# A two-block image kernel with a selective scan: one odd multiply in 16 on VectorE, a later read-out, earlier projection inputs

## The chip, the cores and the metric

The kernel runs on one core of a Trainium2 chip. The metric is the device time of one execution in microseconds; a time is the median of several executions. The engines are TensorE (PE, and PEld for its weight loads), VectorE (DVE), ScalarE (ACT), GpSimd (POOL) and SyncE (SP), which here issues every DMA. Each works through its own instructions in the order of the program, and they meet at semaphores.

## The reference, cut to what matters

Sixteen images of 64 x 64 positions and 96 channels go through two residual blocks, each behind a group norm. The first block resamples, squares and projects. The second one is a selective scan over the 4096 positions, in four directions, of 192 channels with 16 states each:

```python
def step(h, inps):
    dt, ut, bt, ct = inps
    h = jnp.exp(dt[..., None] * As[None]) * h + (dt * ut)[..., None] * bt[:, :, None, :]
    y = jnp.einsum('bkdn,bkn->bkd', h, ct)
    return (h, y)
...
x_dbl = jnp.einsum('bkdl,kcd->bkcl', xs, x_proj_weight)
dts, Bs, Cs = jnp.split(x_dbl, [R, R + N], axis=2)
dts = jnp.einsum('bkrl,kdr->bkdl', dts, dt_projs_weight)
As = -jnp.exp(A_logs).reshape(K, d, N)
ys = selective_scan(xs, dts, As, Bs, Cs, Ds.reshape(K, d), dt_projs_bias)
```

`dt` passes through a softplus first. The whole is in fp32.

## The kernel before, in words

**Three generators around one loop.** `front` (L240) is all that stands ahead of an image's scan: block one, group norms, the depthwise convolution, and the stores of the scan's inputs xs to DRAM. `finish` (L510) is what follows it: norm, gate, output projection. Both are Python generators; each `yield` ends a slice of work. `front(0)` runs by itself before the scan and `finish(15)` after it; all others are woven into the scan loop of another image, slice by slice.

**The scan.** `scan` (L606) goes through 128 steps: 16 images of 8 steps, a step being one pair of directions (forward or backward) and one quarter (T = 1024) of the positions. A step has 6 blocks of 4 pairs, so 24 pairs n; 3072 in all. A pair has two groups, e = 1 (odd) and e = 0 (even), each of 32 channels x 4 states on the 128 partitions. For each pair the loop (from L833 on) issues:

- `recur(n, 1)`: VectorE scans the odd group, reading the decay `da` from PSUM and the drive `b` from SBUF, and writes h over `b` (L740 forward, L742 backward).
- `keep(n, 1)`: ScalarE copies the last column of h for the next quarter (L748; not in the last quarter of a direction).
- `decay(n + 1, 1)`: ScalarE makes the next odd decay in PSUM (L725; two buffers of 128 x 1024 in PSUM, one of each parity).
- `read_out(n - 1)`: TensorE adds both groups of the pair before into y, 16 matmuls (L764), and with the first pair of a block of a backward step also what the forward step left (y0, L757).
- slot 0; then POOL multiplies the odd h by ct in place (L877), and `drive(n + 2)`: POOL multiplies dtu by bt for both groups of the pair after next (L731), into one of three buffers `b`.
- `recur(n, 0)`: VectorE scans the even group, h into PSUM over `da`; slot 1; VectorE multiplies it by ct from PSUM into `b` (L887); `keep(n, 0)`, `decay(n + 1, 0)`, slot 2.

When a block of 4 pairs is over, `store` (L769) copies y out by ScalarE and issues its store.

**The slots.** In each of the three slots of a pair the `Background` class takes at most one slice of two generators: the projection of the next step, and `front` of the next image or, when that is done, `finish` of the last one. Rates are set by SLICES, PSLICES and the number of positions (L72 to L75): the projection goes on by about one slice for each slot, so its 58 slices fill about pairs 0 to 19 of a step. Nothing but program order decides: an instruction of a slice that waits holds up all that its engine has behind it.

**The projection.** `project` (L622) makes the step sizes of the next step in two halves of TB = 512 columns. It loads three tiles u (L634, three buffers), waits three slots, multiplies them into pp (PE, L640), one slot later copies that to pr (ACT, L643), and then goes through three chains, in the order v = 0, 2, 1: s by a matmul (L650), softplus in ScalarE and VectorE (L658 to L669), dtu = s x u[v] (DVE, L672), a copy to delta (ACT, L674), and the stores of dtu and delta to DRAM (L676, L677). `fetch` (L679) loads these again, spread over the partitions, in two buffers each, a block ahead of their use; `fetch_bc` loads bt and ct.

**Other places the change touches.** In `front`, the resampled image s returns from DRAM in two tiles, of 44 and 20 columns, that have SBUF pools of their own (b18 and b12), by six loads (L415), before the loop whose matmuls (L433) use it. In the loop, y0 is fetched (L867, L702; one buffer) in the second pair of a block for the first pair of the next.

Of the kernel before, what the change touches and what calls it, by code (L numbers as in the profile page):

```python
# [45 lines left out]
F32 = mybir.dt.float32  # L46
# [25 lines left out]
SLICES = 540  # L72
WAIT = -1
# [5 lines left out]
def tile_two_blocks(  # L79
# [103 lines left out]
    b12 = ctx.enter_context(tc.tile_pool(name="b12", bufs=1))  # L183
# [56 lines left out]
    def front(mi):  # L240
# [72 lines left out]
        for p0 in range(0, UPS, PP):  # L313
# [94 lines left out]
        JS = 44  # L408
        s = [
            b18.tile([UPS, JS, C], F32, name="s0", tag="b18"), b12.tile([UPS, HW - JS, C], F32, name="s1", tag="b12")  # L410
        ]
        for _ in range(2):
            yield
        for i, n, first in [(0, JS // 4, k * JS // 4) for k in range(4)] + [(1, 10, 0), (1, 10, 10)]:
            nc.sync.dma_start(out=s[i][:, first:first + n, :], in_=s_d[:, JS * i + first:JS * i + first + n, :])  # L415
            yield
# [4 lines left out]
        for j0 in range(0, HW + 8, 8):  # L421
            if done is not None:
                nc.scalar.activation(
                    x1v[:, :, j0 - 8:j0], done.rearrange("c w h -> c h w"), AF.Identity, bias=shift
                )
            if j0 < HW:
                done = bank([C, 8, HW], "e_ps")
                nc.tensor.matmul(
                    done.rearrange("c w h -> c h w"), lhsT=lin, rhs=x1v[:, :, j0:j0 + 8], start=True, stop=False,
                    skip_group_check=True,  # L430
                )
                for j in range(8):
                    nc.tensor.matmul(  # L433
                        done[:, j, :], lhsT=s[(j0 + j) // JS][:, (j0 + j) % JS, :], rhs=down_s, start=False, stop=True,
                        skip_group_check=True,
                    )
            yield
# [168 lines left out]
    def scan():  # L606


        with ExitStack() as es:
# [3 lines left out]
            p3 = es.enter_context(tc.tile_pool(name="sc_3", bufs=3))  # L613
# [8 lines left out]
            def project(mi, pair, lc, out):  # L622
# [6 lines left out]
                xs_d = image[mi]["xs"]  # L629
                for t in range(0, T, TB):  # L630
                    u = []
                    for v in range(3):
                        uv = up_.tile([128, TB], F32, name="u")
                        nc.sync.dma_start(out=uv, in_=xs_d[v, :, lc * T + t:lc * T + t + TB])  # L634
                        u.append(uv)
                    for _ in range(3):
                        yield
# [3 lines left out]
                    yield  # L641
# [4 lines left out]
                    for i, v in enumerate((0, 2, 1)):  # L646
# [30 lines left out]
                        nc.sync.dma_start(out=out["delta"][v][:, t:t + TB], in_=delta)  # L677

            def fetch(what, ctx, bi):  # L679

                v, s0, r = blocks[bi]
                t = p2.tile([128, 2, T], F32, name=what)
                for e in (1, 0):
                    nc.sync.dma_start(
                        out=t[:, e, :],
                        in_=ctx[what][v][32 * (s0 + e):32 * (s0 + e) + 32, :].unsqueeze(1).to_broadcast([32, NQ, T]),
                    )
                return t
# [39 lines left out]
            def drive(n):  # L728
                b = p3.tile([128, 2, T], F32, name="b")
                bt = bc[0, blocks[units[n][1]][2], units[n][2]]  # L730
                nc.gpsimd.tensor_mul(b, ops["dtu", n // NQ], bt.unsqueeze(1).to_broadcast([128, 2, T]))  # L731
                bs[n] = b
# [11 lines left out]
            def keep(n, e, h):  # L744
                st, bi, j = units[n]
                if st % NT < NT - 1:
                    end = h[:, T - 1:T] if steps[st][1] == 0 else h[:, 0:1]
                    nc.scalar.copy(states[bi][1][:, e, j:j + 1], end)  # L748
# [84 lines left out]
            for n, (st, bi, j) in enumerate(units):  # L833
# [19 lines left out]
                if j == 0:  # L853
                    ahead = None
                    if bi + 1 < len(blocks):
                        ahead = ctxs[st], bi + 1
                    elif n + NQ <= last:
                        step_gen.drain()
                        ahead = ctxs[st + 1], 0
                    if ahead:  # L860
                        ops["dtu", m + 1] = fetch("dtu", *ahead)
                elif j == 1:
                    if ahead:
                        ops["delta", m + 1] = fetch("delta", *ahead)
                    if n + NQ <= last and steps[units[n + NQ - 1][0]][1] == 1:
                        st2, bi2, _ = units[n + NQ - 1]
                        y0s[steps[st2][2], bi2] = fetch_y0(steps[st2][2], bi2)  # L867

                h = bs[n][:, 1, :]
                recur(n, 1, h)  # L870
                keep(n, 1, h)
                if n < last:
                    decay(n + 1, 1)
                if n:
                    read_out(n - 1)
                slot(0)
                nc.gpsimd.tensor_mul(h, h, bc[1, r, j])  # L877
# [9 lines left out]
                nc.vector.tensor_mul(bs[n][:, 0, :], h, bc[1, r, j])  # L887
                keep(n, 0, h)
# [16 lines left out]
            read_out(last)  # L905
# [112 lines left out]
```

## Time and profile before

| | |
|---|---|
| median of 3 runs | 21,913.98 us (21,904.93 to 21,924.91) |
| profiled execution | 21,910.69 us |
| its span, first to last instruction | 21,908.9 us |
| POOL, DVE, PE, ACT busy | 95%, 91%, 70%, 60% |
| first and last start of L731 on POOL | 513.3 us and 21,735.6 us |
| DMA traffic | 4276.30 MB, mean 195 GB/s |
| mean granted TensorE clock | 0.766 |

A line of the groups reads: source line, engine, operation, what it writes and from what, shapes and count; then the busy time in us, the mean duration of one in ns, the idle time of the engine just before these instructions, and what ended most of it. A line of the waits reads: who waited, for whom, us in total, how often, and the longest. A line of the timeline reads: start in us, duration, engine, line, instruction, count, and in brackets the idle time before it with its releaser. SPq is the queue of SyncE, where a DMA is issued.

### The profile page before, as it was taken

Reading aid. Unit: us, or ns where it says so; the run is one execution under the profiler, and the core shown is the slowest. Engines: PE = TensorE matmul, PEld = TensorE weight load, DVE = VectorE, ACT = ScalarE, POOL = GpSimd, SP = SyncE. Lnnn points to the kernel's source line nnn. Section 1 sums busy time; section 2 is a strip of 40 time slices with the busy share of each in tenths; the row PEclk is TensorE's granted clock in tenths of the full one; section 3 lists DMA queues with packets and bytes.
Section 4 is the critical chain, followed back from the end, with each engine's and each line's share of the span. In section 5 each row is a group of like instructions: output and inputs, shape, how many; then the busy total and the mean of one; then the engine's idle time right before and its main releaser. Section 6 shows DMA issues by size and latency. Waiting matters only on the chain.

```text
span 21908.9 us, 260666 instructions
## 1 busy us (share of the span) xinstructions
PE 15342.2 (70%) x92844; PEld 6324.7 (29%) x92844; DVE 19849.9 (91%) x12829; ACT 13130.2 (60%) x20854; POOL 20900.4 (95%) x6152
## 2 busy tenths in 40 slices
PE   6766767766777677777767677767777677677745
PEld 4322323232232322324233232322323223242211
DVE  0999999999999999999999999999999999999996
ACT  4665656666565665656656566665656656566543
POOL 0999999999999999999999999999999999999997
PEclk7776777877778777777877778777787877778856
DMA  2555565656656566565655656556565655656654
GB/s 80 190 191 188 193 214 194 209 195 200 205 191 215 189 206 201 192 215 192 207 198 194 214 192 209 196 201 206 193 211 189 210 199 198 206 195 208 210 177 134
DMA packets 1851895, 4276.30 MB, mean 195 GB/s; under 512 B 449118, under 2 KB 548350, under 8 KB 1848542
## 3 DMA queue, kind: packets, MB, share of 16 engines
q1 hardware_dynamic: 1850590, 4259.62, 58.1%
q8 instruction: 731, 11.98, 0.2%
q14 instruction: 574, 4.70, 0.1%
HBM read 3380.58 MB, written 878.18 MB: 194 GB/s over the span
## 4 chain that ended last, share of the span: by engine, by line
DVE 36%; POOL 19%; issue 18%; PE 9%; ACT 9%; DMA 7%; SPq 1%; POOLq 0%; DVEq 0%; ACTq 0%
POOL b L731 10%; POOL b L877 10%; DVE da L742 7%; DVE da L740 7%; DVE b L740 6%; DVE b L742 6%; DVE b L887 4%; ACT da L725 4%; DMA u<-xs_d 2%; DVE s L669 2%; DVE dtu L672 2%; DVE s L668 2%; PE y L764 1%; DMA ct<-rows 1%; PE pp L640 1%
## 5 line engine op out<-in xcount | busy, mean ns | idle before, releaser
L731 POOL TENSOR_TENSOR b<-dtu,bt 128x2048 f32<-128x2048 f32 x3072 | 13984.9, 4552 | 584.6 <-DMA dtu<-dtu_d 522.9
L725 ACT ACTIVATE da<-delta,a_s 128x1024 f32<-128x1024 f32 x6144 | 6853.5, 1116 | 2826.6 <-DVE b L887 1185.9
L877 POOL TENSOR_TENSOR b<-b,ct 128x1024 f32<-128x1024 f32 x3072 | 7309.1, 2379 | 259.8 <-ACT new L748 249.5
L764 PE MATMUL y<-b,fold_s 128*32 128x256 f32 x49152 | 4638.9, 492 | 4107.3 <-DVE b L887 3102.6
L887 DVE TENSOR_TENSOR b<-da,ct 128x1024 f32<-128x1024 f32 x3072 | 3752.6, 1222 | 84.5
L764 PEld LDWEIGHTS y<-b,fold_s 128*32 128x32 f32 x49152 | 1353.3, 126 | 7627.7 <-DVE b L887 4083.3
L740 DVE TENSOR_TENSOR_SCAN da<-da,new,b 128x1024 f32<-128x1024 f32 x1152 | 2694.3, 2339 | 252.3 <-ACT da L725 252.3
L740 DVE TENSOR_TENSOR_SCAN b<-da,new,b 128x1024 f32<-128x1024 f32 x1152 | 2698.0, 2342 | 174.1 <-POOL b L731 166.9
L742 DVE TENSOR_TENSOR_SCAN da<-da,new,b 128x1024 f32<-128x1024 f32 x1152 | 2693.8, 2338 | 172.9 <-ACT da L725 172.7
L742 DVE TENSOR_TENSOR_SCAN b<-da,new,b 128x1024 f32<-128x1024 f32 x1152 | 2697.1, 2341 | 151.6 <-POOL b L731 109.5
L748 ACT COPY new<-da 128x1 f32<-128x1 f32 x2304 | 362.3, 157 | 3028.5 <-DVE b L887 3023.2
L473 PE MATMUL c_ps<-xgp,wtap_s 96*128 96x512 f32 (+1 forms) x4608 | 1817.8, 675 | 168.9 <-ACT row L491 164.1
L650 PE MATMUL s<-pr,dtw_s 128*128 128x512 f32 x1536 | 1120.4, 819 | 557.8 <-ACT delta L674 516.7
L377 PE MATMUL o_ps<-w2c_s,hsq 128*100 128x96 f32 x9600 | 1205.3, 293 | 191.9 <-ACT hsq L348 180.1
L365 PE MATMUL h_ps<-xu,w1t_s 96*128 96x500 f32 x1920 | 1147.6, 700 | 244.2 <-ACT hsq L348 108.6
L748 ACT COPY new<-b 128x1 f32<-128x1 f32 x2304 | 432.6, 188 | 1445.7 <-DVE b L742 740.4
L377 PEld LDWEIGHTS o_ps<-w2c_s,hsq 128*100 128x100 f32 x9600 | 1119.5, 203 | 407.4 <-ACT hsq L348 227.7
L640 PE MATMUL pp<-u,xpt_s 128*128 128x512 f32 x1536 | 903.7, 734 | 224.2 <-DMA u<-xs_d 216.0
L742 DVE TENSOR_TENSOR_SCAN b<-da,b 128x1024 f32<-128x1024 f32 x384 | 876.7, 2283 | 133.2 <-ACT da L725 74.8
L473 PEld LDWEIGHTS c_ps<-xgp,wtap_s 96*128 96x128 f32 (+1 forms) x4608 | 631.9, 182 | 1193.3 <-issue 938.6
L740 DVE TENSOR_TENSOR_SCAN da<-da,b 128x1024 f32<-128x1024 f32 x384 | 875.8, 2281 | 106.9 <-ACT da L725 106.9
L742 DVE TENSOR_TENSOR_SCAN da<-da,b 128x1024 f32<-128x1024 f32 x384 | 876.0, 2281 | 105.0 <-ACT da L725 105.0
(120 smaller groups left out, 18077.1 us busy)
## 6 DMA issues: line engine op xcount, KB each, us to landing
dtu<-dtu_d SPq DMA_DIRECT2D x1536, 512.0 KB
delta<-delta_d SPq DMA_DIRECT2D x1536, 512.0 KB
bt<-rows SPq DMA_DIRECT2D x1024, 512.0 KB
ct<-rows SPq DMA_DIRECT2D x1024, 512.0 KB
u<-xs_d SPq DMA_DIRECT2D x896, 256.0 KB
dtu_d<-dtu SPq DMA_DIRECT2D x768, 256.0 KB
delta_d<-delta SPq DMA_DIRECT2D x768, 256.0 KB
xr<-in_x SPq DMA_DIRECT2D x768, 128.0 KB
```

Source lines behind the costliest of these rows:

```text
L365: nc.tensor.matmul(h_ps[j], lhsT=w1t_s[:, 128 * j:128 * (j + 1)], rhs=xu.rearrange("c p q -> c (p q)"), start=True, stop=True,)
L377: nc.tensor.matmul(o_ps[:, p, :], lhsT=hsq[j][:, UPS * p:UPS * (p + 1)], rhs=w2c_s[:, j, :], start=(j == 0), stop=(j == HB - 1),)
L473: nc.tensor.matmul(c_ps[p:p + n], lhsT=wtap_s[:, tap, 128 * i:128 * i + n], rhs=xgp[:, h0:h0 + 8, dx:dx + HW], start=(tap == 0), stop=(tap ...
L640: nc.tensor.matmul(pp, lhsT=xpt_s[:, pair, v, :], rhs=u[v], start=(v == 0), stop=(v == 2))
L650: nc.tensor.matmul(s, lhsT=dtw_s[:, pair, v, :], rhs=pr, start=True, stop=True)
L725: nc.scalar.activation(da, ops["delta", n // NQ][:, e, :], AF.Exp, scale=a_s[:, k, g, units[n][2]:units[n][2] + 1])
L731: nc.gpsimd.tensor_mul(b, ops["dtu", n // NQ], bt.unsqueeze(1).to_broadcast([128, 2, T]))
L740: nc.vector.tensor_tensor_scan(out, da, b, before, ALU.mult, ALU.add)
L742: nc.vector.tensor_tensor_scan(out[:, ::-1], da[:, ::-1], b[:, ::-1], before, ALU.mult, ALU.add)
L764: nc.tensor.matmul(y[32 * q:32 * q + 32, e, :], lhsT=fold_s, rhs=b[:, e, QT * q:QT * q + QT], start=(pair == 0 and j == 0 and e == 0), sto ...
L877: nc.gpsimd.tensor_mul(h, h, bc[1, r, j])
L887: nc.vector.tensor_mul(bs[n][:, 0, :], h, bc[1, r, j])
```

## The change

In every sixteenth pair (n mod 16 = 15) the odd scan writes h into PSUM, as the even one does, and VectorE multiplies it by ct from there; POOL does it in the other 15. `read_out` and `store` come a pair later (n - 2), with four buffers `b` in place of three. In `project`, the loads of u for the first half are issued at the start, four slots ahead of pp; for the second half each tile is loaded at the end of the chain that used its buffer, and pp follows directly after the last of these; pr comes two slots after pp. The y0 fetch moves to the last pair of the block before. In `front` s comes as 40 and then 24 columns through one buffer, which frees the pool b12. `fetch` issues its two DMAs through a new helper, `spread`; its two buffers were there before. `keep` takes the copying function as an argument, always ScalarE's.

```diff
+SHARE = 16
...
-    b12 = ctx.enter_context(tc.tile_pool(name="b12", bufs=1))
...
+        def fetch_s(first, n):
+            t = b18.tile([UPS, n, C], F32, name="s", tag="b18")
+            for k in range(0, n, 8):
+                nc.sync.dma_start(out=t[:, k:k + 8, :], in_=s_d[:, first + k:first + k + 8, :])
+                yield t, first
+
+        JS = 40
         for _ in range(2):
             yield
-        for i, n, first in [(0, JS // 4, k * JS // 4) for k in range(4)] + [(1, 10, 0), (1, 10, 10)]:
-            nc.sync.dma_start(out=s[i][:, first:first + n, :], in_=s_d[:, JS * i + first:JS * i + first + n, :])
+        for s, s_first in fetch_s(0, JS):
             yield
...
+            if j0 == JS:
+                for s, s_first in fetch_s(JS, HW - JS):
+                    yield
+                for _ in range(2):
+                    yield
...
-            p3 = es.enter_context(tc.tile_pool(name="sc_3", bufs=3))
+            p4 = es.enter_context(tc.tile_pool(name="sc_4", bufs=4))
...
+                order = (0, 2, 1)
+
+                def fetch_u(v, t):
+                    uv = up_.tile([128, TB], F32, name="u")
+                    nc.sync.dma_start(out=uv, in_=xs_d[v, :, lc * T + t:lc * T + t + TB])
+                    return uv
+
+                ahead_u = [fetch_u(v, 0) for v in order]
+                for _ in range(4):
+                    yield
                 for t in range(0, T, TB):
-                    u = []
-                    for v in range(3):
-                        uv = up_.tile([128, TB], F32, name="u")
-                        nc.sync.dma_start(out=uv, in_=xs_d[v, :, lc * T + t:lc * T + t + TB])
-                        u.append(uv)
-                    for _ in range(3):
-                        yield
+                    u, ahead_u = dict(zip(order, ahead_u)), []
                     pp = gps.tile([128, TB], F32, name="pp", tag="g")
                     for v in range(3):
                         nc.tensor.matmul(pp, lhsT=xpt_s[:, pair, v, :], rhs=u[v], start=(v == 0), stop=(v == 2))
-                    yield
+                    for _ in range(2):
+                        yield
                     pr = pj.tile([128, TB], F32, name="pr")
...
                         nc.sync.dma_start(out=out["delta"][v][:, t:t + TB], in_=delta)
+                        if t + TB < T:
+                            ahead_u.append(fetch_u(v, t + TB))
...
-                    if n + NQ <= last and steps[units[n + NQ - 1][0]][1] == 1:
-                        st2, bi2, _ = units[n + NQ - 1]
-                        y0s[steps[st2][2], bi2] = fetch_y0(steps[st2][2], bi2)
-
-                h = bs[n][:, 1, :]
+
+                odd_here = n % SHARE == SHARE - 1
+                h = das[n, 1] if odd_here else bs[n][:, 1, :]
                 recur(n, 1, h)
-                keep(n, 1, h)
+                if odd_here:
+                    nc.vector.tensor_mul(bs[n][:, 1, :], h, bc[1, r, j])
+                keep(n, 1, h, nc.scalar.copy)
                 if n < last:
                     decay(n + 1, 1)
-                if n:
-                    read_out(n - 1)
+                if n >= 2:
+                    read_out(n - 2)
                 slot(0)
-                nc.gpsimd.tensor_mul(h, h, bc[1, r, j])
+                if not odd_here:
+                    nc.gpsimd.tensor_mul(h, h, bc[1, r, j])
                 if n + 2 <= last:
                     drive(n + 2)

                 h = das[n, 0]
                 recur(n, 0, h)
-                if n and units[n - 1][2] == NQ - 1:
-                    storing = store(n - 1)
+                if n >= 2 and units[n - 2][2] == NQ - 1:
+                    storing = store(n - 2)
                     next(storing)
...
+                if j == NQ - 1 and n < last and steps[units[n + 1][0]][1] == 1:
+                    st2, bi2, _ = units[n + 1]
+                    y0s[steps[st2][2], bi2] = fetch_y0(steps[st2][2], bi2)
```

More of the change, by code (lines that the diff above doesn't have):

```diff
@@ L405, in front @@
         stow(sd, UPS - 2 * PG)
[L408 to L411, printed above, removed]
+        def fetch_s(first, n):
[4 more added lines that the diff above has]
+        JS = 40
         for _ in range(2):
             yield
-        for i, n, first in [(0, JS // 4, k * JS // 4) for k in range(4)] + [(1, 10, 0), (1, 10, 10)]:
-            nc.sync.dma_start(out=s[i][:, first:first + n, :], in_=s_d[:, JS * i + first:JS * i + first + n, :])
+        for s, s_first in fetch_s(0, JS):
             yield
@@ L433, in front @@
                     nc.tensor.matmul(
-                        done[:, j, :], lhsT=s[(j0 + j) // JS][:, (j0 + j) % JS, :], rhs=down_s, start=False, stop=True,
+                        done[:, j, :], lhsT=s[:, j0 + j - s_first, :], rhs=down_s, start=False, stop=True,
                         skip_group_check=True,
@@ L640, in project @@
                         nc.tensor.matmul(pp, lhsT=xpt_s[:, pair, v, :], rhs=u[v], start=(v == 0), stop=(v == 2))
-                    yield
+                    for _ in range(2):
+                        yield
                     pr = pj.tile([128, TB], F32, name="pr")
                     nc.scalar.activation(pr, pp, AF.Identity, bias=bumps_s)
-                    for i, v in enumerate((0, 2, 1)):
+                    for i, v in enumerate(order):
                         if i == 0:
@@ L677, in project, with spread @@
                         nc.sync.dma_start(out=out["delta"][v][:, t:t + TB], in_=delta)
+                        if t + TB < T:
+                            ahead_u.append(fetch_u(v, t + TB))
+            def spread(out, what, ctx, bi, e):
+                v, s0, r = blocks[bi]
+                nc.sync.dma_start(
+                    out=out,
+                    in_=ctx[what][v][32 * (s0 + e):32 * (s0 + e) + 32, :].unsqueeze(1).to_broadcast([32, NQ, T]),
+                )
             def fetch(what, ctx, bi):
-                v, s0, r = blocks[bi]
                 t = p2.tile([128, 2, T], F32, name=what)
                 for e in (1, 0):
[L684 to L687, printed above, removed]
+                    spread(t[:, e, :], what, ctx, bi, e)
                 return t
@@ L728, in drive @@
             def drive(n):
-                b = p3.tile([128, 2, T], F32, name="b")
+                b = p4.tile([128, 2, T], F32, name="b")
                 bt = bc[0, blocks[units[n][1]][2], units[n][2]]
@@ L742, in recur, with keep @@
                     nc.vector.tensor_tensor_scan(out[:, ::-1], da[:, ::-1], b[:, ::-1], before, ALU.mult, ALU.add)
-            def keep(n, e, h):
+            def keep(n, e, h, copy):
                 st, bi, j = units[n]
@@ L747, in keep @@
                     end = h[:, T - 1:T] if steps[st][1] == 0 else h[:, 0:1]
-                    nc.scalar.copy(states[bi][1][:, e, j:j + 1], end)
+                    copy(states[bi][1][:, e, j:j + 1], end)
             def read_out(n):
@@ L887, in scan @@
                 nc.vector.tensor_mul(bs[n][:, 0, :], h, bc[1, r, j])
-                keep(n, 0, h)
+                keep(n, 0, h, nc.scalar.copy)
                 if n < last:
@@ L904, in scan @@
                         bc[what, 0, ahead_j] = fetch_bc(ctxs[st + 1], 0, ahead_j, what)
-            read_out(last)
+            for n in (last - 1, last):
+                read_out(n)
             for _ in store(last):
```

## The prediction

> **What bounds the kernel now.** I read the busy table first, then the costliest groups, then the waits by engine, then the timeline of one projection.
>
> ```profile
> PE 15342.2 (70%) x92844; PEld 6324.7 (29%) x92844; DVE 19849.9 (91%) x12829; ACT 13130.2 (60%) x20854; POOL 20900.4 (95%) x6152
> ...
> L731 POOL TENSOR_TENSOR b<-dtu,bt 128x2048 f32<-128x2048 f32 x3072 | 13984.9, 4552 | 584.6 <-DMA dtu<-dtu_d 522.9
> ...
> L877 POOL TENSOR_TENSOR b<-b,ct 128x1024 f32<-128x1024 f32 x3072 | 7309.1, 2379 | 259.8 <-ACT new L748 249.5
> ...
> L887 DVE TENSOR_TENSOR b<-da,ct 128x1024 f32<-128x1024 f32 x3072 | 3752.6, 1222 | 84.5
> ```
>
> GpSimd (POOL) is 95% busy, VectorE (DVE) 91%. In the timeline POOL's starts follow each other by 4.49 us after a drive (L731) and 2.31 us after a multiply (L877): 6.80 us for a pair, 163.2 us for the 24 pairs of a step. The scan runs from POOL's first drive at 513.3 us to its last multiply at 21,745.4 us: 21,232 us, or 165.9 us for each of 128 steps. POOL's waits after its start (the page's 844 us less the 512.3 us before the first drive) are some 320 us, 2.5 a step. So POOL sets the pace, but VectorE is only a little behind, as its waits tell:
>
> ```profile
> DVE da L740 <- ACT da L725: 359.2, 285, 5.9
> ...
> DVE da L742 <- ACT da L725: 277.6, 267, 2.4
> ...
> DVE b L740 <- POOL b L731: 216.8, 270, 1.1
> DVE b L742 <- POOL b L731: 166.5, 198, 1.1
> DVE b L742 <- ACT da L725: 114.8, 90, 1.5
> ```
>
> Only 216.8 + 166.5 = 383 us (3.0 a step) of VectorE's idle time is a wait for POOL. ScalarE (ACT) is waited for longest: with the projection's own small waits some 920 us inside the scan (7.2 a step). Laid out by place in the step, the waits for POOL stand in pairs 0 to 3, where no projection runs; in pairs 4 to 20 VectorE trails by 1 to 4 us. POOL's 249.5 us for L748 are also ACT's lateness: the end states of those scans were copied 3.7 us late at the median, where 0.2 us is usual.
>
> The next fence, of one step, shows how an ACT wait arises:
>
> ```profile
> 5052.51 0.59 ACT L674 COPY delta<-s 128x512 f32<-128x512 f32 x1 [0.93 <-DVE dtu L672]
> ...
> 5053.51 2.77 SPq L634 DMA_DIRECT2D u<-xs_d  x3
> ...
> 5064.26 4.90 PE L640 MATMUL pp<-u,xpt_s 128*128 128x512 f32 x6 [5.98 <-DMA u<-xs_d]
> ...
> 5069.19 0.69 ACT L643 ACTIVATE pr<-pp,bumps_s 128x512 f32<-128x512 f32 x1 [4.01 <-PE pp L640]
> ...
> 5074.27 2.36 DVE L740 TENSOR_TENSOR_SCAN da<-da,new,b 128x1024 f32<-128x1024 f32 x1 [3.52 <-ACT da L725]
> ```
>
> The three u tiles were issued behind the delta store and landed about 10.7 us after the first issue. TensorE (PE) stood at pp, pr (ACT) stood 4.01 us, and the even group's scan lost 3.52 us. Over all 768 loads u lands 6.7 us after its issue at the median (5.1 to 9.0 for the middle 80%); the DMA share in this stretch is 0.95.
>
> [...]
>
> **The change, part by part.**
>
> 1. *Odd multiply, 192 of 3072 pairs.* POOL loses 192 x 2.31 = 443 us (3.5 a step). VectorE gains 192 x 1.222 = 235 us (1.8 a step). The multiply runs before the even scan, so that scan and all of VectorE's queue stand 1.22 us later, and at that place POOL gets 2.31 + 1.22 = 3.5 us closer to VectorE. The PSUM buffer is held 1.22 us longer; its next decay (1.12 us) still has 2.34 + 1.22 us before it is needed: nothing. Were VectorE to take over as the bound at once, with ACT's waits unchanged, the most that is left is 383 - 235 = 148 us. Part of the 383 will stay, since in pairs 20 to 3 VectorE (5.9 us a pair of its own) outruns POOL's 6.8: 8 x 0.9 = 7.2 us to catch up, of which the lag now takes about 3 and, with POOL 3.5 us closer, up to 4.5. I keep 1.0 us a step, 128 us (bounds 0 and 190). Gain: 20 us (148 down to -42).
>
> 2. *Read-out two pairs back, four buffers.* PE no longer stops at read_out for L887 (3102.6 us of idle PE) and L877 (989.8). PE has room, so this counts only where ACT then waits for PE and VectorE for ACT. For every ACT-caused wait of VectorE I looked 7 us back for a wait of ACT on PE: 198 us stand behind pr, 80 behind the projection's s, 103 behind the other background matmuls; 509 us have no such wait, ACT is simply full, and stay. Of the 80 + 103 = 183 I take 155 (bounds 60 and 300, the latter with pr). The drive still needs the buffer whose read-out stands in the same pair of the program, so POOL does not get further ahead.
>
> 3. *u a chain ahead.* For the first half of a step four slots instead of three, and pr two slots after pp: its wait goes. That wait (118 of the 198 us) stands in pair 2, where VectorE otherwise waits for POOL: nothing. For the second half only two of the three tiles come early. The third chain's load stands behind the last delta store, with pp directly after it: no slot between where there were three, and pr two slots on instead of four. Relative to the end of pair 10's odd scan the delta copy moves from -5.2 us (pair 9) to about +1.9 (it is then queued behind a decay), the issue is at +2.3, the landing at +2.3 + 6.5 = 8.8, and the remaining four pp matmuls (4.90/6 = 0.82 us each after a wait, 0.59 otherwise) end at 11 to 12. Pr's place comes at +7.0, as now. So ACT stands 4 to 5 us where the mean is now 0.8. In the steps of now where pr stood 3.5 to 3.9 us the next even scan lost 3.0 to 3.5; over all steps it loses 1.15 there. Cost: 2.1 us a step, 270 us (bounds 40, if the load lands in some 4 us, and 450, if the read-out queued behind pp holds drives too).
>
> 4. *Step sizes.* They were in two buffers before (bufs=2); the new helper issues the same two DMAs: nothing, up or down.
>
> 5. *y0 fetch at the pair before its use.* SP waited 128.7 us for its buffer and no longer will; SP runs ahead. Nothing (bounds -20 and +20).
>
> 6. *The s image in 40 + 24 columns of one buffer.* Fifteen of 16 times beside the scan. Before the scan once: a second load with nothing beside it, about 6 us (first load: issued at 259.0, used at 263.5, with 15.4 us of waits). SP's queue stands behind it, two pairs at most. Four slots more for an image, of some 520 in 540: fits.
>
> Sum against the profiled execution's 21,910.7 us (span 21,908.9 and 1.8 around it): -20 - 155 + 270 + 6 = +101, so 22,012 us. The median of the runs shown is 21,914.0, 3 us above the profiled one, less than I can tell.
>
> **Rivals.**
>
> - *Faster.* The third load lands under cover and the freed PE gives most of its waits back: -148 + 64 (half a step's residue) - 250 + 60 + 6 = -268, so 21,643 us. One mechanism decides: whether u of the last chain lands within 4.5 us of its issue; then pr is in time. For it: two thirds of the competing u loads are gone by then. Against it: landings of 6.7 us and a DMA share of 0.95.
> - *Even.* Stall of 1.5 us a step (190) and all 183 back: -20 - 183 + 190 + 6 = -7: 21,904 us.
> - *Much slower.* PE stuck at pp holds the read-out too, POOL's drive waits for the buffer: -148 + 190 - 60 + 384 + 6 = +372, so 22,283 us. For it: in the two latest landings of now POOL's drive did wait 1.8 and 2.1 us. Against it: in all, POOL waits 15.9 us for the read-out.
> - *Not what it says.* "Step sizes in double buffers" changes nothing; inside every case.
>
> **Chances.** My forecast (21,955 to 22,200) 0.45; faster (21,500 to 21,866) 0.27; even, within 44 us, 0.14; much slower 0.14. About 0.2% is what a measurement of this kernel can tell from no change. Range 21,680 to 22,300: beyond it lie the better half of the faster case and the end of the slowest, some 0.18. Faster 0.27, same 0.14, slower 0.59.
>
> **What would show it.** POOL's L877 group has 2880 instructions, near 6,850 us; a new VectorE group of 192 takes 1.22 us. Step 1 is right if VectorE's waits for POOL fall from 383 to about 130 us; step 2 if PE's wait for L887 at the read-out nearly vanishes and ACT's waits on s and the other matmuls shrink; step 3 if pr still waits 450 us or more in all (444.8 now), and nearly all of it in the second half of a step, with PE's pp waiting longer for u than 216 us. If pr's wait falls below 200 us, or VectorE's waits for ACT below 700, the forecast is wrong and the faster case holds.

## The result, and the profile after

The changed kernel takes 22,429.74 us (median of 4 runs, 22,415.47 to 22,436.17), the kernel before beside it 21,914.98 (4 runs): ratio 1.0234, interval 1.0216 to 1.0252, 515 us slower. The forecast was 22,012 us with a range up to 22,300; the direction was right, the time lies outside the range. The span of the profiled execution after is 22,426.6 us.

Busy time and the groups that answer to those shown of before:

```profile
PE 15375.0 (69%) x92844; PEld 6500.3 (29%) x92844; DVE 20147.6 (90%) x13021; ACT 13139.6 (59%) x20854; POOL 20469.9 (91%) x5960
...
L748 POOL TENSOR_TENSOR b<-dtu,bt 128x2048 f32<-128x2048 f32 x3072 | 13898.2, 4527 | 1034.9 <-DMA dtu<-dtu_d 516.9
...
L895 POOL TENSOR_TENSOR b<-b,ct 128x1024 f32<-128x1024 f32 x2880 | 6789.4, 2357 | 753.6 <-ACT new L765 612.8
...
L905 DVE TENSOR_TENSOR b<-da,ct 128x1024 f32<-128x1024 f32 x3072 | 3753.2, 1222 | 85.0
```

L748 is the drive (L731 before), L895 POOL's multiply (L877), L905 VectorE's (L887). The odd multiply moved as foreseen: 2880 on POOL, and 192 on VectorE. POOL is busy for 430 us less, yet the span is 518 us longer: POOL waits about 950 us more. The idle time ahead of its drives rose from 584.6 to 1034.9 us, that ahead of its multiplies from 259.8 to 753.6. Who was waited for, from POOL's waits before and then after:

```profile
POOL b L877 <- ACT new L748: 249.5, 168, 4.0
POOL b L731 <- PE y L764: 15.9, 17, 2.5
```

```profile
POOL b L895 <- ACT new L765: 612.8, 474, 4.7
...
POOL b L748 <- PE y L781: 513.4, 154, 12.8
```

The last line is the new one: a drive that waits for a read-out, up to 12.8 us at a time. Laid out by place in the step, 404 of the 513 us stand in pair 11. VectorE's waits after:

```profile
DVE da L757 <- ACT da L742: 506.6, 299, 14.4
...
DVE da L759 <- ACT da L742: 157.3, 165, 2.0
DVE b L757 <- POOL b L748: 124.9, 167, 1.1
DVE b L759 <- POOL b L748: 113.1, 152, 1.1
```

In the first line the longest wait grew from 5.9 to 14.4 us. VectorE waits less for POOL (252 us in all, 383 before) and more for ScalarE. The timeline of one step, the fourth of an image, shows both stalls at once:

```profile
5182.94 2.07 PE L651 MATMUL pp<-u,xpt_s 128*128 128x512 f32 x2 [6.44 <-ACT delta L686]
...
5185.35 0.34 SPq L689 DMA_DIRECT2D delta_d<-delta  x1
5186.58 0.32 SPq L641 DMA_DIRECT2D u<-xs_d  x1
...
5195.08 3.78 PE L651 MATMUL pp<-u,xpt_s 128*128 128x512 f32 x4 [10.07 <-DMA u<-xs_d]
...
5198.65 1.91 PE L435 MATMUL e_ps<-xt,lin 96*96 96x512 f32 x2
...
5198.90 0.69 ACT L655 ACTIVATE pr<-pp,bumps_s 128x512 f32<-128x512 f32 x1 [10.76 <-PE pp L651]
...
5201.97 1.07 PE L781 MATMUL y<-b,fold_s 128*32 128x256 f32 x16
...
5203.15 4.52 POOL L748 TENSOR_TENSOR b<-dtu,bt 128x2048 f32<-128x2048 f32 x1 [12.74 <-PE y L781]
...
5207.16 2.36 DVE L757 TENSOR_TENSOR_SCAN da<-da,new,b 128x1024 f32<-128x1024 f32 x1 [14.41 <-ACT da L742]
```

Read it from the top. The first two matmuls of pp waited 6.44 us for the delta copy, which held their PSUM buffer. The third tile of u was issued at 5186.58, behind the delta store; the remaining four matmuls began 8.5 us later. TensorE ran no matmul in the 10.07 us ahead of them. The matmuls of L435 and then the read-out (L781) stood behind pp: they began at 5198.65 and 5201.97, though VectorE and POOL had finished the read-out's inputs by 5190.50. In this trace images 2 to 14 begin their 5802 matmuls each in one and the same order, and likewise their 812 instructions on VectorE, 1303 on ScalarE and 372 on POOL. The read-out frees the buffer `b` that POOL's next drive writes: POOL stood for 12.74 us. ScalarE stood 10.76 us at pr, and VectorE 14.41 us for a decay.

The fourth step is the worst of an image. Over the 127 steps whose second half lies inside the scan, the third tile of u landed 3.9 us after its issue at the median (3.1 to 7.9 us for the middle 80%), in 88 of them within 4.5 us; in the fourth steps it took 8.1 us at the median.

### The profile page after: what moved, and what is told of

Same layout as the page of the kernel before. It is cut to its first block, busy times and chain, and to the rows that moved or that the text cites. A ratio compares the mean times of both kernels' runs of the same rounds, so it can differ in the third digit from the quotient of the medians.

```text
span 22426.6 us, 259622 instructions
## 1 busy us (share of the span) xinstructions
PE 15375.0 (69%) x92844; PEld 6500.3 (29%) x92844; DVE 20147.6 (90%) x13021; ACT 13139.6 (59%) x20854; POOL 20469.9 (91%) x5960
## 5 line engine op out<-in xcount | busy, mean ns | idle before, releaser
L748 POOL TENSOR_TENSOR b<-dtu,bt 128x2048 f32<-128x2048 f32 x3072 | 13898.2, 4527 | 1034.9 <-DMA dtu<-dtu_d 516.9
L895 POOL TENSOR_TENSOR b<-b,ct 128x1024 f32<-128x1024 f32 x2880 | 6789.4, 2357 | 753.6 <-ACT new L765 612.8
L781 PE MATMUL y<-b,fold_s 128*32 128x256 f32 x49152 | 4259.4, 478 | 1155.7 <-DVE b L905 657.1
L905 DVE TENSOR_TENSOR b<-da,ct 128x1024 f32<-128x1024 f32 x3072 | 3753.2, 1222 | 85.0
L757 DVE TENSOR_TENSOR_SCAN da<-da,new,b 128x1024 f32<-128x1024 f32 x1232 | 2883.0, 2340 | 444.3 <-ACT da L742 435.0
L759 DVE TENSOR_TENSOR_SCAN da<-da,new,b 128x1024 f32<-128x1024 f32 x1232 | 2881.2, 2339 | 110.5 <-ACT da L742 105.5
L781 PEld LDWEIGHTS y<-b,fold_s 128*32 128x32 f32 x49152 | 1508.6, 129 | 4265.3 <-issue 1512.3
L757 DVE TENSOR_TENSOR_SCAN b<-da,new,b 128x1024 f32<-128x1024 f32 x1072 | 2510.9, 2342 | 164.1 <-POOL b L748 113.0
L759 DVE TENSOR_TENSOR_SCAN b<-da,new,b 128x1024 f32<-128x1024 f32 x1072 | 2509.6, 2341 | 112.2 <-POOL b L748 112.0
L651 PE MATMUL pp<-u,xpt_s 128*128 128x512 f32 x1536 | 1210.6, 927 | 1062.0 <-DMA u<-xs_d 641.3
L480 PE MATMUL c_ps<-xgp,wtap_s 96*128 96x512 f32 (+1 forms) x4608 | 1734.6, 640 | 165.3 <-ACT row L498 160.8
L774 PE MATMUL y<-y,ident_s 128*128 128x512 f32 x768 | 593.5, 865 | 953.8 <-ACT yt L792 767.8
L377 PE MATMUL o_ps<-w2c_s,hsq 128*100 128x96 f32 x9600 | 1109.2, 278 | 166.4 <-ACT hsq L348 123.0
L377 PEld LDWEIGHTS o_ps<-w2c_s,hsq 128*100 128x100 f32 x9600 | 1031.5, 189 | 378.5 <-ACT hsq L348 177.0
L324 PE MATMUL u_ps<-up_s,xr 64*64 64x25 f32 x12288 | 661.1, 260 | 455.8 <-ACT t L335 242.8
```

The lines of the kernel that those rows point to most:

```text
L377: nc.tensor.matmul(o_ps[:, p, :], lhsT=hsq[j][:, UPS * p:UPS * (p + 1)], rhs=w2c_s[:, j, :], start=(j == 0), stop=(j == HB - 1),)
L480: nc.tensor.matmul(c_ps[p:p + n], lhsT=wtap_s[:, tap, 128 * i:128 * i + n], rhs=xgp[:, h0:h0 + 8, dx:dx + HW], start=(tap == 0), stop=(tap ...
L651: nc.tensor.matmul(pp, lhsT=xpt_s[:, pair, v, :], rhs=u[v], start=(v == 0), stop=(v == 2))
L757: nc.vector.tensor_tensor_scan(out, da, b, before, ALU.mult, ALU.add)
L759: nc.vector.tensor_tensor_scan(out[:, ::-1], da[:, ::-1], b[:, ::-1], before, ALU.mult, ALU.add)
L781: nc.tensor.matmul(y[32 * q:32 * q + 32, e, :], lhsT=fold_s, rhs=b[:, e, QT * q:QT * q + QT], start=(pair == 0 and j == 0 and e == 0), sto ...
```

## The experiments

Each kernel ran beside the kernel before on the same chip. Differences below are between medians. The executions of one kernel spread over 10 to 50 us, so a difference under some 25 us between two of them is not told from none.

**Theory 1**: the cost is the projection, by TensorE's queue. pp of the second half stands directly behind the chain and waits for u; the read-out behind it holds POOL's drives. **Rival 2**: ScalarE's stand at pr is the cost, whatever TensorE does. **Rival 3**: other parts cost it: the later read-out, the s image, or the share.

### One part at a time

e1 is the kernel before with the diff's part in `project` alone; e2 with the part in `front` alone (s in 40 + 24 columns); e3 with the odd multiply alone; e4 is the changed kernel with `project` of before; e5 is e4 without the odd multiply.

e4 against the changed kernel, and the lines of e4 that e5 takes back:

```diff
-                ahead_u = [fetch_u(v, 0) for v in order]
-                for _ in range(4):
-                    yield
                 for t in range(0, T, TB):
-                    u, ahead_u = dict(zip(order, ahead_u)), []
+                    u = []
+                    for v in range(3):
+                        uv = up_.tile([128, TB], F32, name="u")
+                        nc.sync.dma_start(out=uv, in_=xs_d[v, :, lc * T + t:lc * T + t + TB])
+                        u.append(uv)
+                    for _ in range(3):
+                        yield
...
-                    for _ in range(2):
-                        yield
+                    yield
...
-                        if t + TB < T:
-                            ahead_u.append(fetch_u(v, t + TB))
```

```diff
-                odd_here = n % SHARE == SHARE - 1
-                h = das[n, 1] if odd_here else bs[n][:, 1, :]
+                h = bs[n][:, 1, :]
...
-                if odd_here:
-                    nc.vector.tensor_mul(bs[n][:, 1, :], h, bc[1, r, j])
...
-                if not odd_here:
-                    nc.gpsimd.tensor_mul(h, h, bc[1, r, j])
+                nc.gpsimd.tensor_mul(h, h, bc[1, r, j])
```

> The kernel before with the changed projection alone: u tiles at the ends of the chains, pp directly after the last of them, pr two slots after pp. Theory 1 (the late third u load holds TensorE at pp, and what stands behind it with it): this part alone carries most of the loss, 22,150 to 22,350 us, POOL's wait for the read-out rises from 16 to over 300 us. Theory 2 (the s image in two loads through one buffer jams the DMA queue): no more than 22,000 us here. Theory 3 (VectorE has become the bound through the odd multiply): 21,914 within 40 us.

> The kernel before with s in 40 and 24 columns through one buffer alone. Theory 1: 21,920 to 21,990 us. Theory 2: over 22,100 us, with the excess in the fourth step of each image, where the loop over s lies. Theory 3: 21,914 within 40 us.

> The kernel before with one odd multiply in 16 on VectorE alone. Theories 1 and 2: 21,770 to 21,920 us, since POOL loses 443 us and VectorE gains 235. Theory 3: 22,000 us or more, with VectorE's waits for POOL near nothing and POOL's waits for VectorE's scans over 200 us.

> The changed kernel with the projection of before (three u loads three slots ahead of pp, pr one slot after it). Theory 1: most of the loss goes, 21,800 to 22,000 us, POOL's wait for the read-out back under 60 us. Theory 2: 22,250 us or more. Theory 3: 22,300 us or more.

> The kernel before with s in 40 and 24 columns (which makes the room), four buffers b, the read-out and the store a pair later and the y0 fetch moved; no multiply is moved and the projection is the old one. If the later read-out by itself frees ScalarE: 21,780 to 21,900 us, below the 21,971 us of the s image alone. If it gives nothing: 21,950 to 21,990 us, and the gain of the changed kernel with the old projection comes from the moved multiply beside it.

| kernel | median us | ratio to before (95%) |
|---|---|---|
| e1, projection alone | 22,391.30 | 1.0216 (1.0201 to 1.0232) |
| e2, s image alone | 21,970.93 | 1.0024 (1.0014 to 1.0033) |
| e3, odd multiply alone | 21,927.77 | 1.0005 (0.9997 to 1.0014) |
| e4, all but the projection | 21,845.87 | 0.9967 (0.9955 to 0.9979) |
| e5, e4 without the odd multiply | 21,867.74 | 0.9978 (0.9968 to 0.9987) |

The projection alone costs nearly all; everything else together is a gain. The steps in order: s image +55 us (e2), read-out later -103 (e5 against e2), odd multiply beside it -22 (e4 against e5), projection +584 (the changed kernel against e4). They add up to +514, as they must, since each step starts where the last one ended; the sum is no test. The projection costs 476 us alone (e1) and 584 beside the other parts. Rival 3 falls, but for the 55 us.

e1 lies above its expected range, and its trace puts only 4.8 us of POOL's waits to the read-out, where over 300 were expected. The rest stands under another name:

```profile
POOL b L738 <- issue: 333.0, 82, 11.2
```

81 of these 82 waits end within 0.2 us of the last matmul of a read-out, so they are taken for the same wait. In e4 it is 156.2 us, where under 60 were expected: with the later read-out some of it stays in every kernel.

e3, 8 us above its range, tells where POOL's saved 430 us went. These are two of its waits:

```profile
POOL b L882 <- ACT new L749: 512.0, 420, 5.2
...
POOL b L732 <- PE y L765: 41.3, 31, 3.8
```

POOL's multiply overwrites h, so it needs the copy of the end state (L749) first. With less work POOL comes sooner to it and waits 512 us there, where it waited 249.5. More than half of what it saved is given back at this one place, and the time does not move. (Another 77.5 us stand under "issue", 11.2 before.) VectorE's waits for POOL fell from 383 to 197 us. At these places ScalarE's copies set the pace.

In e2, seven of the eight steps of an image keep their length within 0.8 us (means over all images but the first and the last); the seventh grew from 165.3 to 168.5, which is 3.2 x 16 = 51 of the 55 us. Beside it `finish` runs, which starts four slots later since `front` has four more, and the wait of pr for pp grew there from 1.95 to 7.35 us a step. Whether this is the cause no run tells; e7 below speaks against the wait at pr by itself. The mean granted TensorE clock was lower too, 0.754 beside 0.766, but most of all in the fifth step (0.815 beside 0.870, means over all images), which is no longer.

### What stands behind pp

e6 puts three slots ahead of pp in the second half, so that the late load can land; e7 leaves pp where it is and takes pr two slots later; e8 leaves both and loads all three tiles at least a chain ahead, with a fourth buffer u. In this order:

```diff
+                    for _ in range(3 if t else 0):
+                        yield
                     pp = gps.tile([128, TB], F32, name="pp", tag="g")
...
-                    for _ in range(2):
+                    for _ in range(1 if t else 2):
                         yield
```

```diff
-                    for _ in range(2):
+                    for _ in range(4 if t else 2):
                         yield
```

```diff
-            up_ = es.enter_context(tc.tile_pool(name="sc_u", bufs=3))
+            up_ = es.enter_context(tc.tile_pool(name="sc_u", bufs=4))
...
+                    if t + TB < T:
+                        ahead_u.append(fetch_u(order[0], t + TB))
...
-                        if t + TB < T:
-                            ahead_u.append(fetch_u(v, t + TB))
+                        if t + TB < T and i < 2:
+                            ahead_u.append(fetch_u(order[i + 1], t + TB))
```

> The changed kernel, in the second half of a projection with three slots between the last u load and pp, and one from pp to pr; the loads stay where they are. Theory 1 (TensorE held at pp, and the rest behind it): 21,800 to 21,950 us. If the places of the loads in the DMA queue are the cause, and not pp's: over 22,250 us.

> The changed kernel with pp still directly after the last u load, but pr four slots after pp in the second half. If what costs is TensorE's queue behind pp (read-out and with it POOL's drives, s, the front's matmuls): 22,200 to 22,430 us, though ScalarE's wait at pr falls from 376 us to under 150. If it is ScalarE's stop at pr: 21,850 to 22,000 us.

> The changed kernel with a fourth u buffer, so that each of the three loads for the second half, the last one too, is issued a chain (eight slots) or more before pp; pp and pr stay where they are. Theory 1: 21,760 to 21,860 us, below the 21,846 us of the changed kernel with the old projection or level with it, TensorE's wait for u under 150 us. Otherwise, if the earlier loads only push other loads back: over 21,950 us.

| kernel | median us | ratio to before (95%) |
|---|---|---|
| e6 | 22,124.58 | 1.0096 (1.0081 to 1.0112) |
| e7 | 22,491.32 | 1.0265 (1.025 to 1.028) |
| e8 | 22,020.65 | 1.0048 (1.0033 to 1.0063) |

e7 bears on rival 2. ScalarE's wait at pr in the changed kernel and in e7, then POOL's in e7 and e8:

```profile
ACT pr L655 <- PE pp L651: 376.4, 105, 13.8
```

```profile
ACT pr L655 <- PE pp L651: 24.6, 10, 13.9
```

```profile
POOL b L748 <- PE y L781: 451.8, 139, 15.2
```

```profile
POOL b L750 <- PE y L783: 126.0, 87, 2.9
```

In e7 pr no longer waits, and the kernel is no faster. POOL's wait for the read-out stayed. So pr's place is not the cost. But ScalarE was not set free: in the same step as above it now stands at the next product of TensorE behind pp, one of block one, and VectorE after it. From e7's timeline:

```profile
5218.38 0.68 ACT L425 ACTIVATE xt<-e_ps,shift 96x512 f32<-96x512 f32 x1 [13.59 <-PE e_ps L440]
...
5219.45 4.52 POOL L748 TENSOR_TENSOR b<-dtu,bt 128x2048 f32<-128x2048 f32 x1 [12.38 <-PE y L781]
...
5223.46 2.36 DVE L757 TENSOR_TENSOR_SCAN da<-da,new,b 128x1024 f32<-128x1024 f32 x1 [14.05 <-ACT da L742]
```

e8 takes away the wait for the late tile itself: POOL's wait for the read-out falls to 126.0 us, VectorE's for the forward decays from 506.6 to 301.2, and 409 us of time are gone. So the cost is the load directly ahead of pp, through what stands behind pp in TensorE's queue. Whether the read-out, which holds POOL, or the products for ScalarE, which hold VectorE's decays, set the time was not separated: no run frees one of the two alone. By the steps of an image the changed kernel is 0.5, 3.7, 2.4, 10.3, 2.8, 0.7, 2.6 and 3.5 us longer than e8. In the second step POOL's wait for the read-out grew by 0.3 us and VectorE's for ScalarE by 3.4; in the first the read-out's grew by 2.2 and the step by 0.5. The read-out alone therefore does not account for it.

All three missed their expected times. e6 and e7 have two slices more than the others: the chains of their second half stand two slots later, and the last stores run at the head of pair 20. So neither is a clean test of the slots. What that costs can be estimated from e10 and e13 below: e6 is 268 us above e10, 182 of it from the first half, so some 86 us are the second half's. Without them e7 would still take some 22,405 us, 25 below the changed kernel. e8 is clean, and 175 us slower than e4. Something else in the projection costs.

### The places of before

e9 is e8 with three slots, pp, one slot, pr in both halves, so that every chain stands where it stood before. e10 is the same with the late third load (e6 without its surplus). e11 is e9 with pp moved directly behind the chain and pr left in place. First e9 and e10 (against e8 and the changed kernel), then e11 against e9:

```diff
-                for _ in range(4):
-                    yield
                 for t in range(0, T, TB):
+                    for _ in range(3):
+                        yield
...
-                    for _ in range(2):
-                        yield
+                    yield
```

```diff
-                    for _ in range(3):
+                    for _ in range(0 if t else 3):
...
-                    yield
+                    for _ in range(4 if t else 1):
+                        yield
```

> The changed kernel with four buffers u and all three loads of the second half at least a chain ahead, as in e8, and with the places of before in each half: three slots, pp, one slot, pr (58 places in all, so each chain stands at the same pair as before). Theory 1 (what e8 still lost, 175 us against e4, is the place of the matmul pp directly behind a chain, where it waits for the delta copy that holds its PSUM buffer, and the first half's chains two slots later): 21,780 to 21,860, no slower than e4's 21,846. Rival (loading ahead itself costs, since the loads stand among those of dtu and delta): 21,960 to 22,040, as e8.

> The changed kernel with its own loads (three buffers, the third load of the second half behind the last delta store) and the places of before: three slots, pp, one slot, pr, 58 places. This is e6 without the two places too many. Theory 1 (the late load costs nothing once three slots stand between it and pp): 21,820 to 21,900, POOL waits for the read-out under 60 us. Rival (the place of the load in the DMA queue is the cost): over 22,100.

> As e9, but in the second half pp stands directly behind the chain, and pr four slots after it, so that all three chains of each half stay at the places of e9: pp's place alone is moved. Theory 1a (pp waiting behind the delta copy is what e8 still lost): 60 to 180 us above e9. Theory 1b (the first half's chains two slots later are): within 40 us of e9.

| kernel | median us | ratio to before (95%) |
|---|---|---|
| e9 | 21,758.17 | 0.9926 (0.9911 to 0.994) |
| e10 | 21,856.94 | 0.9972 (0.9961 to 0.9984) |
| e11 | 21,767.55 | 0.993 (0.9915 to 0.9945) |

e9 beats both kernels, and its expectation: 161 us below before. e10 shows that the late load itself is cheap: with three slots between it and pp it costs 99 us against e9, and nothing against e4 (11 us). Directly ahead of pp it cost 409. e11 shows that pp's wait for the delta copy is harmless by itself: TensorE waits 427.7 us there, as in e8 (431.3), and the time is e9's. POOL still waits 149.7 us for the read-out in e10, as in e4 (156.2), where under 60 were expected of it too. What is left of e8's loss to try is that the first half's chains stand two slots later.

### The chains one, two, three slots later

Against e9, with d = 1 in e12, 2 in e13, 3 in e14:

```diff
-                    for _ in range(3):
+                    for _ in range(3 - d if t else 3 + d):
                         yield
```

> As e9, with one slot moved from the second half to the first: four slots, pp, one, pr in the first half, two, pp, one, pr in the second. The first half's chains alone stand one slot later. If it is lateness that costs (e8: two slots later, +263 us against e9), some 130 us above e9; if it is which chain meets which pair, any value from 0 to 260 is open.

> As e9, with two slots moved to the first half (five, pp, one, pr; then one, pp, one, pr): the first half's chains stand where e8 and the changed kernel have them, and pp has a slot between it and the chain ahead. If the chains' place is what e8 lost, as e8: 21,980 to 22,060. If pp close behind the chain with pr two slots on is, as e9: under 21,800.

> As e9, with three slots moved to the first half (six, pp, one, pr; then pp at once, one, pr): the first half's chains stand one whole pair later, each slice at the same one of a pair's three slots as in e9. If the slot within a pair decides, near e9 but for pr, which now stands one slot behind a pp that waits (up to 100 us): under 21,880. If lateness decides, over 22,100.

| kernel | median us | against e9 | ratio to before (95%) |
|---|---|---|---|
| e12 | 21,833.42 | +75 | 0.9964 (0.9951 to 0.9977) |
| e13 | 21,940.55 | +182 | 1.0011 (1.0005 to 1.0018) |
| e14 | 21,939.59 | +181 | 1.0011 (1.0002 to 1.002) |

The place of these chains is worth 182 us in e13; the 80 us between e13 and e8 are then pp one slot earlier in each half, in the second half directly behind the chain with pr two slots on. But the cost neither grows in step with the lateness nor vanishes at a whole pair: both theories fall. It sits in some steps only: e13's steps of an image (means over the same images) last 4.1, 4.1 and 3.8 us longer than e9's in the first, second and fourth, and 1.2 in the sixth; the fifth is 1.6 shorter, the others are as long. These are steps with slices of `front` that meet the chains. In the first one VectorE's timeline shows what they meet (POOL's beneath it), both of e13:

```profile
1884.48 6.20 DVE L236 TENSOR_TENSOR nb<-nmean,rg 96x1 f32<-96x1 f32 x1
1890.61 1.21 DVE L906 TENSOR_TENSOR b<-da,ct 128x1024 f32<-128x1024 f32 x1
```

```profile
1883.89 2.33 POOL L896 TENSOR_TENSOR b<-b,ct 128x1024 f32<-128x1024 f32 x1
1886.19 4.48 POOL L749 TENSOR_TENSOR b<-dtu,bt 128x2048 f32<-128x2048 f32 x1
```

A product of 96 x 1 elements lasts 6.20 us and ends with POOL's drive (1886.19 + 4.48 = 1890.67). In e9 the same one lasts 0.49 us: it starts half a microsecond ahead of the end of POOL's multiply (1880.91 + 2.35 = 1883.26) and ends with it. The difference stands in the busy time of this group, 109.4 us in e13 and 23.6 in e9; the waits ahead of it are 299.2 and 299.9 us. The same product lasts 5.8 to 6.2 us in e8, e12, e14 and the changed kernel, and 0.49 in e4, e10 and e11.

### One small operation in VectorE's queue

e15 is e13 with nb made by ScalarE, e16 the changed kernel and e17 e9 with the same edit. e18 is e15 with `lin`, the next sum of two SBUF operands, made in PSUM first. The edit of e15, e16 and e17, then what e18 adds:

```diff
-        nc.vector.tensor_mul(nb, nmean, rg)
+        nc.scalar.activation(nb, nmean, AF.Identity, scale=rg)
```

```diff
-        nc.scalar.activation(lin, mt_s, AF.Identity, scale=rg)
+        lin_ps = bank([C, C], "lin_ps")
+        nc.scalar.activation(lin_ps, mt_s, AF.Identity, scale=rg)
...
-        nc.vector.tensor_add(lin, lin, ident_s[0:C, 0:C])
+        nc.vector.tensor_add(lin, lin_ps, ident_s[0:C, 0:C])
```

> e13 with one instruction moved: the 96x1 product nb (line 236, both inputs in SBUF) is made by ScalarE instead of VectorE. In e13's trace nb takes 6.20 us once an image, in the first step of the image, ending with POOL's drive, where e9's takes 0.49 us. If that wait is what the first step loses (4.1 us of 16 images), 55 to 75 us below e13: 21,865 to 21,886. Rival (the 6.2 us are hidden in VectorE's slack, and the first step is late for ScalarE's sake): within 20 us of e13's 21,941.

> The changed kernel with nb made by ScalarE, as in e15, and nothing else. The same wait of 6.20 us is in its trace, and its first step is as long (166.8 us, e4's 162.4): 55 to 75 us below the changed kernel, 22,355 to 22,375. Rival: no change, 22,410 to 22,440.

> e9 with nb made by ScalarE. Here nb takes 0.49 us in the first step and 1.06 us in the fourth, so little is to be had: 21,735 to 21,765 (e9: 21,758).

> e15 with one edit more: the 96x96 tile lin is made in PSUM, so that the sum of line 259 has one input there. e15 showed the long operation handed on: in its trace nb is gone from VectorE and lin takes 7.69 us once an image (1.28 in e9). If VectorE loses these 6 us because both inputs are in SBUF while GpSimd works, no operation of the first step is long now, the first step falls from 167.3 us to about 163, and the whole is 60 to 75 us below e15's 21,982 (e13: 21,941): 21,865 to 21,925. Rival (the first step is late for another reason and VectorE only shows it): within 20 us of e15.

| kernel | median us | ratio to before (95%) |
|---|---|---|
| e15 | 21,981.84 | 1.0022 (1.0011 to 1.0033) |
| e16 | 22,439.05 | 1.0232 (1.0217 to 1.0248) |
| e17 | 21,753.21 | 0.9925 (0.991 to 0.994) |
| e18 | 21,831.76 | 0.9962 (0.9948 to 0.9976) |

e15 and e16 missed: no gain. Six of e15's eight executions took 21,981 to 21,992 us and two 21,938 to 21,939, so at best it is level with e13. VectorE's groups tell why; e13, e15 and e18 in this order:

```profile
L236 DVE TENSOR_TENSOR nb<-nmean,rg 96x1 f32<-96x1 f32 x32 | 109.4, 3420 | 299.2 <-ACT rg L233 299.2
...
L259 DVE TENSOR_TENSOR lin<-lin,ident_s 96x96 f32<-96x96 f32 x16 | 11.2, 701 | 0.0
```

```profile
L259 DVE TENSOR_TENSOR lin<-lin,ident_s 96x96 f32<-96x96 f32 x16 | 115.6, 7223 | 0.0
```

```profile
L260 DVE TENSOR_TENSOR lin<-lin_ps,ident_s 96x96 f32<-96x96 f32 x16 | 3.9, 244 | 0.0
```

With nb gone, lin took over the wait: 7.22 us in the mean instead of 0.70 (7.7 us once an image, in e16 too). With one operand of lin in PSUM it takes 0.24 us, the first step falls from 167.3 us (e15) to 159.9, and e18 is 150 us faster than e15 and 109 faster than e13, more than the 60 to 75 expected against e15. So this form of operation, meeting POOL at the wrong moment once an image, costs e13 about 110 us. Not all of that belongs to the shift: the first step of e9 lasts 162.4 us, so 66 of the 182 us (4.1 us of 16 images) are lost there by the later chains, and some 40 more are what e9 itself still pays for nb and lin. No run takes both off e9. The rest of the 182, some 116 us net, comes from the second, fourth and sixth steps; in the second and fourth ScalarE makes VectorE wait longer, and the cause was not tried.

## Why the prediction was wrong, point by point

**Step 3, the projection, failed, in two terms.** It was put at 270 us and measured 584.

*The late load was followed along one path only.* The prediction followed it to pr and from there to VectorE's next scan, 2.1 us a step. e8 puts the late load at 409 us, 3.2 us a step, inside the step's bounds of 40 and 450 but not where it was put. It was not the landing: 6.5 us after the issue was forecast, and the median was 3.9. Nor was it pr: its wait was 376.4 us, less than the 450 asked for (362 of it in the second half, as foreseen, with pp waiting 641.3 us for u), and e7, where it is 24.6, is no faster. What the step left out is everything else behind pp in TensorE's queue: the read-out, with POOL's drives behind it (513.4 us of waits, 126.0 in e8), and the products of `front` and `finish` that ScalarE waits for (13.59 us at xt in the step of e7 shown). The first of these entered as the upper bound and as the rival "much slower", with the argument against it that POOL waited 15.9 us for read-outs before. That number was no evidence: before, three slots stood between the loads and pp. The second did not enter. In the first timeline of the changed kernel both are seen: the last four matmuls of pp begin at 5195.08 and last 3.78 us in all, those of L435 and L781 begin behind them, at 5198.65 and 5201.97. The 2.1 us a step took in the wait of pp's own consumer and not that of what stands behind pp.

*The moved slots were priced at nothing.* "For the first half of a step four slots instead of three, and pr two slots after pp: its wait goes" is true of the wait (0.9 us after, 333 before) and left out that all three chains of that half move by two slots. This costs 182 us (e13 against e9), of which 66 us are traced to one small product in VectorE's queue and the rest is open; pp one slot earlier costs 80 more (e8 against e13); loading ahead, where the slots are left alone, gains 88 (e9 against e4). With the 409: 409 + 182 + 80 - 88 = 583; these are steps of one way from e4 to the changed kernel, so the sum is no test.

**Step 1, within its bounds.** Forecast -20 us (bounds -148 to +42); +12 alone (interval -7 to +31), so no gain that can be told, and -22 beside the later read-out. The counts and durations came out (2880 multiplies of POOL, 192 of VectorE of 1.225 us, group L887). VectorE's waits for POOL fell to 197 us in e3, not to the 130 that was to show the step right, and POOL spent more than half of its saving waiting for ScalarE's end-state copies.

**Step 2, about right in size, not by the waits that it named.** Forecast -155 (bounds -60 to -300), measured -103, or -125 with step 1 where both are in. TensorE's 3102.6 us behind L887 at the read-out became 657.1 behind L905, as foreseen. But the step counted on ScalarE's waits for s and the other matmuls and left pr to the upper bound. From e2 to e5 it was the wait at pr that fell, from 518.5 to 136.5 us; that for s went from 164.7 to 129.8, and that for e_ps rose from 170.0 to 210.7.

**Steps 4 and 5** were priced at nothing. Neither was run alone: the y0 fetch is inside the -103, and the helper, which issues the same two DMAs, inside the -22. **Step 6 failed in size**: +6 forecast, 55 measured (e2). "Four slots more for an image ... fits" counted whether they fit, not what `finish` meets when it starts four slots later.

The error of 413 us is then 139 (409 instead of 270), 175 (slots and loads ahead), 49 (s image) and 50 (steps 1 and 2: -125 instead of -175). One sum of the prediction is off without bearing on this: POOL's waits after its start are 332 us (844 less 512), not some 320.

**The rivals.** "Much slower" named one part of the mechanism, and its 384 us for the held drives lie near the 387 by which POOL's wait for the read-out fell in e8; that its sum came nearest is in part luck, since it had no term for the moved slots. "Faster" let one thing decide, whether u landed within 4.5 us. It did in 88 of 127 steps, and the kernel was slower all the same. "Even" had the stall at 1.5 us a step; the late load cost 3.2, and 10.3 in the fourth step of an image.

## What to carry to other kernels

When a wait is moved in an engine's queue, price what stands behind it and who waits for that, not only the consumer of the waiting instruction: here freeing that consumer changed nothing (e7), and freeing the queue gave 409 us (e8). A small wait of today is no evidence on a place that did not exist today. One step's timeline can be the worst of its kind: here the fourth step of an image lost 10.3 us and the others 0.5 to 3.7. Where background work is woven in by slots, count every slice that a changed number of slots moves; here two slots were worth 182 us, and keeping the old places turned a loss of 2.3% into a gain of 0.3% (e10), with all loads a chain ahead 0.7% (e9).

## What the runs showed of the hardware that was not expected

Two VectorE operations with both inputs in SBUF lasted, inside the scan, until an instruction of POOL beside them ended, small as they were. The product of 96 x 1 elements took 0.155 us before the scan. In the scan it took 0.49 to 1.3 us where it began 0.5 to 1.3 us before the end of a multiply of POOL, and ended with that multiply (all 30 of them in the kernel before); in the changed kernel (15 of 30), as in e13, it took 6.20 us where it began 0.6 us after the start of one, the rest of that multiply and the whole drive behind it. The sum lin of 96 x 96 elements took 0.245 us before the scan. In the kernel before it began 1.2 us before the end of a drive, ended with it and lasted 1.28 us; in e15 it began 0.8 us before the end of a drive and lasted 7.7 us, to the end of the drive after the next multiply. So such an operation outlasted the POOL instruction that it met in e13 and e15, and not in the kernel before. What decides how many are sat out, the runs do not show. With one input in PSUM the same sum took 0.244 us in the mean of all 16 (e18). The profile counts these times as busy time of VectorE (109.4 us for nb in e13), and with nb moved to ScalarE the mean of lin went from 0.70 to 7.22 us (e15).
